# Two attentions around a routed expert layer on one core: start-up work as table steps, and keys and values of two more batches computed in the gaps between stages

## The chip, the cores and the metric

The kernel runs on one core of one Trainium2 chip. A core has five engines with instruction streams of their own: PE (matrix multiply; loading its weights is shown apart, as PEld), DVE (vector work along rows, which reads PE's results), ACT (functions, copies and scalings), POOL (a slower general engine, which also issues the indirect gathers and scatters), and SP (which issues transfers and computes nothing). Data sits in on-chip memory by partitions (up to 128 rows); PE writes its results to a small separate memory, PSUM, from which ACT or DVE copies them. Engines wait for each other through semaphores, and each engine runs its own instructions strictly in the order in which they were written into its stream.

The metric is device time in microseconds (us) of the whole program. Every time below is in microseconds from the start of the span, unless it says otherwise.

## The reference

There are 8 batches (B) of 112 rows (S) and 256 columns (D). Each batch has a context of 375 rows (SK). Four blocks follow each other, each added to x:

```
x = x + attention0(layernorm(x), ctx)        # 16 heads of 16, biases, softmax over 375 keys
x = x + experts(layernorm(x))                # router by distance in a ball, 2 of 8 experts per row
x = x + attention1(layernorm(x), ctx, mask)  # 16 heads, mask over 112 x 375, own weights
x = x + ffn(layernorm(x))                    # ternary weights, 1024 wide, convolution over 3 rows, silu

c_proj   = project_to_ball(centroids)
dot      = x_hyper @ c_proj.T
diff_sq  = max(x_norm_sq + c_norm_sq - 2 dot, 0)
arg      = 1 + 2 diff_sq / ((1 - x_norm_sq) (1 - c_norm_sq) + EPS)
top_v, top_i = top_k(-arccosh(arg), 2);   weights = softmax(top_v)
```

Two points matter for the change. The keys and values of both attentions are products of the same context with weights of each layer: `k1 = ctx @ Wk1`, `v1 = ctx @ Wv1` do not depend on x. They can be computed at any time once the context and the weights are on the chip. And the projected centroids and their norms depend on inputs alone.

## The kernel before

**Stages.** The kernel has four stages, one after the other, all in one instruction stream per engine. (1) Loads, and the attention of layer 0 with the router, for eight batches. (2) The experts: the routed rows lie sorted by expert in device memory (`tok`), and 19 tiles of 128 rows go through the two products of their expert (function `run`); the results go back to device memory (`ysc`). (3) The attention of layer 1; per batch it first gathers the two expert results of each row (`Gg0`, `Gg1`, L655) and adds them to x (`Dc0`, `Dc1`, L662). (4) The last feed-forward block.

**Steps and tables.** `attention(layer, ...)` (L622) defines the work of one batch as small named steps. The first letter of a name is the engine: P, D, A, G (POOL), S (SP). For one batch the order of data is: row statistics `Dbn`, `Dba`, `Grt`; normalisation `Dn` (L285); transposes `Ptn` (L703); queries `Ptq` (L716); keys `Pk0`, `Pk1` (L743, four matmuls each) with their copies `Aka0`, `Aka1`; values `Pv0` to `Pv2` (L763, four each in the trace) with copies `Ava0` to `Ava2` into the values' buffer; scores `Ps0` to `Ps3` (L789); the row maximum of the scores, `Dm00` to `Dm31` (L799 in layer 0, and L805 with the mask added in layer 1); then the scores once more in transposed form `Pp0` to `Pp2` (L842, L849), in layer 1 with the mask added by DVE (`Da00` to `Da21`, L860); the exponentials `Ae..` on ACT (L872); the weighted sums `Pw0`, `Pw1` (L887); and the output projection `Pto` to `Pout` (L936) with the addition to x, `Dx` (L940). Layer 0 goes on with the router's steps (`Drn`, `Ptg`, ..., `Dind`, `Prank`, `Drow`, `Gsc0`, `Gsc1`).

The order in which the engines get these steps is written out by hand in the table `ORDER`, one list per layer. An entry is a name, a time, and the first and last batch. Times are in units of one batch: a step with time t of batch b stands at b + t. The steps are sorted by that and issued:

```
plan = sorted((b + t, i, b, n) for i, (n, t, b0, b1) in enumerate(ORDER[layer]) for b in range(b0, b1 + 1))
with tc.manual_schedule(engines={ET.PE, ET.DVE, ET.Activation, ET.Pool}):
    for _, _, b, n in plan:
        do[n](b)
```

Inside it, PE, DVE, ACT and POOL take their instructions in just this order. SP is not in the list: its transfers are placed by the scheduler. So a step that waits for its data holds everything that the table puts behind it on its engine.

**Keys and values ahead.** `key_value(mark, batch, lay)` (L737) makes the steps of one batch's keys and values. With the mark `X0` and `X1` (`AHEAD = 2`) it makes those of layer 1 for batches 0 and 1; the table of layer 0 issues them near its end, with its last batch (7). Layer 1 computes the others, batches 2 to 7, in its own table (`Pk0 ... 2, 7`). The pool of keys and the list of values' buffers `vbuf` have three entries each; the buffers of values are filled with ones once, on POOL (L230), because each head's sum of weights comes out of such a column. The two small PSUM banks that hold keys, values, queries and transposes are handed out in turn by `misc`.

**Start.** Before the table of layer 0 the kernel issues, in program order, the loads (x and context of each batch by turns on SP, weights on ACT's queue), constants on POOL and DVE, the fills of the values' buffers, and the projection of the centroids (L303 to L316: one square, two matmuls, an inverse root, some ten small DVE steps). The mask's load is behind all of them on SP; DVE scales it by 1/16 (L997), a constant that the scheduler puts between the table's steps.

**Other work in the tables.** `Dtb0`, `Dta0`, `Ptc0`, `Dtc0`, `Dtd0`, `Dte0`, `Dtf0` (and the same with 1) make the ternary weights of the last block from loaded weights; the buffers of these raw weights are needed by two of the expert weights' loads, so those loads wait for `Dtf0` and `Dtf1`. `Sld` and `Slo` load layer 1's attention weights. `Glt0` to `Glt7` in layer 1's table build the convolution's diagonal matrices on POOL (L1111).

**The passage to the experts.** After the table of layer 0 come the last weights of the router and `rt.further()` (L526), which counts how many rows each expert has (L529) and picks the experts of the last tiles on DVE; with these, SP fetches the first tiles of rows (`tn`, L1033), which PE transposes (L1039).

## Time and profile before

| | us |
|---|---|
| median of three runs | 617.55 (617.51 to 618.69) |
| the profiled execution, its own time | 619.23 |
| span of the profiled execution | 617.5 |
| PE busy | 552.3 (89%) |
| DVE busy | 352.3 (57%) |
| ACT busy | 260.0 (42%) |
| POOL busy | 96.1 (16%) |

| stage, from its borders in the trace | from | to |
|---|---|---|
| loads, constants, first scores | 0 | about 30 |
| layer 0's attention and router in full swing | 30 | 190 |
| end of the router, count, first fetch (215.50) | 190 | 218 |
| experts | 218 | 362 |
| first gather (365.22), start of layer 1's attention | 362 | 410 |
| layer 1's attention | 410 | 538 |
| last block | 538 | 617.5 |

How to read it: the profile shows one execution. A line of the stage view gives, for a stretch of time, its length, and how long PE, PEld, DVE, ACT and POOL were busy in it (in brackets the number of instructions), then the mean granted clock of PE as a share of full speed, the busy share of the transfer engines and what they moved in GB/s. A line of the waits names an engine and its instruction, what it waited for, and the total, number and longest of these waits. A line of the timeline gives start, length, engine, line, operation, result and operands, and in square brackets how long the engine was idle before it and what it waited for. In the 40 slices each digit is a busy share in tenths of a slice of 15.4 us.

### The profile page before, as it was taken

What the parts mean: (1) busy time and instruction counts of PE and PEld (TensorE: products, weight loads), DVE (VectorE), ACT (ScalarE), POOL (GpSimd) and SP (SyncE); (2) the same over time, 40 slices, a digit from 0 to 9 for tenths busy, and PEclk for the clock granted to TensorE, in tenths of its full rate; (3) what the DMA queues carried; (4) which work ended last, traced back from release to release, by engine and by line L of the source; (5) the groups of instructions that cost most, each with busy time, mean ns of one, the idle gap of its engine ahead of it and who ended that gap; (6) DMA issues with size and microseconds to landing.
All of it is one profiled execution on the core that took longest, in us unless ns stands there. A gap on an engine that the chain in (4) does not pass through costs nothing. (4 is left out here: it accounts for less than half of the span.)

```text
span 617.5 us, 13564 instructions
## 1 busy us (share of the span) xinstructions
PE 552.3 (89%) x5402; PEld 418.5 (68%) x5402; DVE 352.3 (57%) x1093; ACT 260.0 (42%) x560; POOL 96.1 (16%) x185
## 2 busy tenths in 40 slices
PE   2799999999997689999999947799999999799983
PEld 1456666766685489998999934366666666588872
DVE  4464666787867601111111126889999989836653
ACT  1245565456462143333343311165454554554430
POOL 5000101223335300000000025323101201200000
PEclk9999999999999879999999985599999999989996
DMA  9999800021301039988889711000000000000000
GB/s 280 375 362 341 324 1 1 10 85 51 103 17 48 30 116 335 332 301 305 338 333 335 310 41 39 15 17 15 4 16 3 1 3 2 1 2 16 15 16 15
DMA packets 35916, 76.49 MB, mean 124 GB/s; under 512 B 3100, under 2 KB 29708, under 8 KB 30988
## 3 DMA queue, kind: packets, MB, share of 16 engines
q1 hardware_dynamic: 32940, 70.73, 32.2%
q0 software_dynamic: 1536, 3.67, 1.9%
q10 hardware_dynamic: 1376, 1.21, 0.7%
q8 instruction: 43, 0.70, 0.5%
q14 instruction: 21, 0.17, 0.1%
HBM read 55.68 MB, written 19.92 MB: 122 GB/s over the span
## 5 line engine op out<-in xcount | busy, mean ns | idle before, releaser
L1056 ACT ACTIVATE hT<-t_h,we 128x128 f32<-128x128 f32 x152 | 55.6, 368 | 82.0 <-PE t_h L1052 77.0
L1052 PEld LDWEIGHTS t_h<-tnT,we 128*128 128x128 f32 x608 | 80.1, 196 | 6.0 <-issue 0.6
L1052 PE MATMUL t_h<-tnT,we 128*128 128x128 f32 x608 | 83.5, 282 | 0.3 <-DMA we<-in_WA_dram 0.2
L799 DVE TENSOR_REDUCE topf<-pair 112x2 f32<-112x750 f32 x64 | 58.0, 930 | 36.1 <-PE pair L789 36.1
L789 PE MATMUL pair<-k,q 32*112 32x375 f32 x512 | 70.5, 551 | 5.5 <-DVE topf L799 3.2
L1063 PE MATMUL t_y<-we,hT 128*128 128x256 f32 x304 | 75.2, 380 | 0.0
L805 DVE CUSTOM_DVE_ANT_0 sm<-pair,mask 112x375 f32<-112x375 f32 x128 | 63.0, 540 | 7.9 <-PE pair L789 7.4
L842 PE MATMUL pair<-q,k 32*125 32x224 f32 x768 | 57.4, 376 | 1.1 <-DVE pT L860 0.8
L1063 PEld LDWEIGHTS t_y<-we,hT 128*128 128x128 f32 x304 | 53.3, 191 | 4.9
L860 DVE TENSOR_TENSOR pT<-pair,mask 125x896 f32<-125x896 f32 x48 | 50.6, 1085 | 7.1 <-PE pair L849 6.9
L763 PE MATMUL bank<-wv,ctx 128*125 128x256 f32 x192 | 51.8, 401 | 0.5 <-ACT k L756 0.3
L743 PE MATMUL bank<-ctx,wk 128*128 128x375 f32 x128 | 51.3, 526 | 0.0
L872 ACT ACTIVATE pT<-pair 125x896 f32<-125x896 f32 x48 | 42.5, 920 | 15.3 <-PE pair L849 15.1
L1041 DVE COPY tnT<-t_tn 128x256 f32<-128x256 f32 x19 | 8.1, 424 | 70.7 <-PE t_tn L1039 63.6
L682 POOL TENSOR_SCALAR rs<-mv 112x1 f32<-112x1 f32 x32 | 7.6, 237 | 251.4 <-DVE mv L676 204.6
L763 PEld LDWEIGHTS bank<-wv,ctx 128*125 128x125 f32 x192 | 33.3, 188 | 19.6 <-issue 6.7
L872 ACT ACTIVATE pT<-pT 125x896 f32<-125x896 f32 x48 | 45.6, 954 | 1.5 <-DVE pT L860 1.4
L887 PE MATMUL bank<-pT,v 125*32 125x112 f32 x1536 | 43.4, 261 | 0.0
L1065 DVE TENSOR_TENSOR y<-t_y,we 128x256 f32<-128x256 f32 x19 | 8.1, 425 | 60.1 <-PE t_y L1063 60.1
L1218 PE MATMUL t_c<-hpad,taps 128*128 128x224 f32 x192 | 40.5, 360 | 1.9 <-DVE hpad L1209 1.9
L842 PEld LDWEIGHTS pair<-q,k 32*125 32x125 f32 x768 | 31.4, 182 | 15.0 <-issue 4.4
L655 POOL DMA_INDIRECT yg<-ysc,at x16 | 16.7, 1045 | 156.6 <-SPq L1095 153.3
(206 smaller groups left out, 813.8 us busy)
## 6 DMA issues: line engine op xcount, KB each, us to landing
we<-in_WB_dram SPq DMA_DIRECT2D x19, 1152.0 KB, 7.2
we<-in_WA_dram SPq DMA_DIRECT2D x19, 1028.0 KB, 5.3
tok<-zero SPq DMA_DIRECT2D x8, 896.0 KB, 9.8
ysc<-zero SPq DMA_DIRECT2D x8, 896.0 KB, 10.6
ctx<-in_ctxT_dram SPq DMA_DIRECT2D x8, 375.0 KB, 5.8
tn<-tok SPq DMA_DIRECT2D x19, 128.0 KB, 5.9
ysc<-y SPq DMA_DIRECT2D x19, 128.0 KB, 3.0
we<-in_w1T_dram SPq DMA_DIRECT2D x1, 1024.0 KB, 7.6
```

What stands on the lines that cost most here:

```text
L743: nc.tensor.matmul(t, wts[lay]["k"][:, c, o * 128 : (o + 1) * 128], ctx_t[batch(b)][:, c, :], start=(c == 0), stop=(c == 1),)
L763: nc.tensor.matmul(t, ctx_t[batch(b)][:, c, i * KC : (i + 1) * KC], wts[lay]["v"][:, c, :], start=(c == 0), stop=(c == 1),)
L789: nc.tensor.matmul(ts[j // 2][:S, j % 2, :SK], q[r, c, i, :], k[r, c, :], start=True, stop=True)
L799: nc.vector.tensor_reduce(top[:, g, 2 * m : 2 * m + 2], t[:S, :, :SK], AX.X, ALU.max, negate=True)
L805: nc.vector.tensor_tensor_reduce(out=sm, in0=t[:S, n, :SK], in1=mask_t, scale=-1.0, scalar=3.0e38, op0=ALU.add, op1=ALU.min, accum_out=top ...
L842: nc.tensor.matmul(ts[j // 2][:KC, j % 2, n * 2 * S : (n + 1) * 2 * S], k[r, c, i * KC : (i + 1) * KC], q[r, c].rearrange("p i s -> p (i s)"),
L860: nc.vector.tensor_tensor(pT, st[b][f"p{s}"][m][:KC, :, : 4 * S], mask2[:, lo : lo + 4 * S].unsqueeze(1).to_broadcast([KC, 2, 4 * S]), ALU ...
L872: nc.scalar.activation(pT, src, AF.Exp)
L887: nc.tensor.matmul(po[32 * j : 32 * j + 32, g, :], v[:, i, h, :], st[b][f"T{s}{r // 2}"][:, r % 2, lo : lo + S], start=(i == 0), stop=(i = ...
L1052: nc.tensor.matmul(ph[:, i, :], w1[:, c, f * 128 : (f + 1) * 128], nt[:, c, :], start=(c == 0), stop=(c == 1),)
L1056: nc.scalar.activation(hT[:, f, :], ph[:, i, :], AF.Gelu, bias=b1[:, f : f + 1])
L1063: nc.tensor.matmul(py, hT[:, f, :], w2[:, f, :], start=(f == 0), stop=(f == NF - 1))
```

## The change

It has five parts.

1. **Four buffers.** `NKV = 4` keys and values are kept in place of three.
2. **Two more batches ahead.** `AHEAD = 3`: layer 1's keys and values of batch 2 (steps `PX2..` and `AX2..`) are issued on PE and ACT after `rt.further()`, in a manual schedule of their own, at the end of stage 1. Those of batch 3 (`PY..`, `AY..`) become the first steps of layer 1's table. The steps `Pk0` to `Ava2` of that table run over batches 4 to 7.
3. **Centroids as steps.** Their projection is taken apart into `Dce0`, `Pce`, `Dce1`, `Dce2`, `Dce3` of layer 0's table; their PSUM tile comes out of `misc`.
4. **Fills as steps.** The fill of each values' buffer is a step `Gms` (four of them, all before the first `Grt` on POOL).
5. **Both tables written anew.** All times in `ORDER` differ. Statistics of batches 0 to 5 stand ahead of the first normalisation; `Dbn2`, `Dba2`, `Grt2` come right after `Dx` in layer 0; the ternary steps `Dtf1` and `Dtf0` go from 7.76 and 6.67 to 9.52 and 9.93; in layer 1, gathers, normalisation and queries stand further ahead of the scores. A tile of statistics has a tag per batch.

The diff, the tables cut to rows that the text speaks of:

```diff
+NKV = 4
...
 ORDER = [
     [
-        ("Dbn", -0.7765, 0, 7), ("Dba", -0.7547, 0, 7), ("Grt", -0.6335, 0, 7), ("Dn", -0.5744, 0, 7),
-        ("Ptn", -0.4938, 0, 7), ("AnT", -0.4537, 0, 7), ("Dtb1", -0.0374, 4, 4), ("Pk0", 0.0988, 0, 7),
-        ("Aka0", 0.1715, 0, 7), ("Ptq", 0.1943, 0, 7), ("Pk1", 0.2299, 0, 7), ("Aq0", 0.2348, 0, 7),
...
-        ("Ae20", 2.6258, 0, 7), ("Ae21", 2.6435, 0, 7), ("Pw0", 2.6710, 0, 7), ("Au0", 2.7427, 0, 7),
-        ("Dtf1", 2.7640, 5, 5), ("Gxb", 2.8424, 0, 7), ("Pw1", 2.9085, 0, 7), ("Au1", 3.0470, 0, 7),
...
-        ("AoT", 3.4147, 0, 7), ("Dte0", 3.5660, 3, 3), ("Pout", 3.6431, 0, 7), ("Dtf0", 3.6728, 3, 3),
-        ("Dx", 3.7361, 0, 7), ("Dbn2", 3.7658, 0, 7), ("Dba2", 3.8311, 0, 7), ("Grt2", 3.9219, 0, 7),
-        ("PX0k0", 4.0016, 7, 7), ("Drn", 4.0321, 0, 7), ("AX0ka0", 4.1799, 7, 7), ("Ptrn", 4.2797, 0, 7),
...
-        ("Dwt3", 8.1115, 0, 6), ("PX1v0", 8.3020, 7, 7), ("Dwt4", 8.9238, 0, 6), ("PX0v1", 9.1727, 7, 7),
-        ("AX1va0", 9.9255, 7, 7), ("PX1v1", 9.9306, 7, 7), ("AX0va1", 10.9247, 7, 7), ("PX1v2", 12.5746, 7, 7),
-        ("AX1va2", 13.3041, 7, 7), ("AX1va1", 13.3187, 7, 7),
+        ("Gms", -13.7779, 0, 3), ("Dbn", -6.4648, 0, 7), ("Dba", -4.7943, 0, 7), ("Dce0", -1.7910, 0, 0),
+        ("Pce", -1.7313, 0, 0), ("Grt", -1.4128, 0, 7), ("Dn", -1.0660, 0, 7), ("Dce1", -0.9077, 0, 0),
+        ("Dce2", -0.8237, 0, 0), ("Ptn", -0.5250, 0, 7), ("AnT", -0.4788, 0, 7), ("Dbv", -0.3448, 0, 0),
+        ("Pk0", 0.0228, 0, 7), ("Aka0", 0.1009, 0, 7), ("Ptq", 0.1418, 0, 7), ("Aq0", 0.1524, 0, 7),
+        ("Aq1", 0.1538, 0, 7), ("Dtb1", 0.1883, 4, 4), ("Pk1", 0.2718, 0, 7), ("Aka1", 0.3455, 0, 7),
...
+        ("Dce3", 3.5143, 0, 0), ("Pout", 3.6425, 0, 7), ("Dta0", 3.8385, 2, 2), ("Dtd0", 3.8469, 3, 3),
+        ("Dx", 3.8562, 0, 7), ("Dbn2", 3.8849, 0, 7), ("Dba2", 3.9033, 0, 7), ("Sld", 3.9228, 7, 7),
...
+        ("Dte0", 4.4070, 3, 3), ("Ptxh", 4.5004, 0, 7), ("Dtf1", 4.5188, 5, 5), ("PX0k1", 4.6075, 7, 7),
...
+        ("AX0va2", 6.7018, 7, 7), ("Gsc0", 6.7050, 0, 7), ("Gzp", 6.7086, 0, 6), ("Dtf0", 6.9259, 3, 3),
...
+        ("AX1ka1", 11.1606, 7, 7), ("PX1v0", 12.6658, 7, 7), ("AX0va1", 15.1426, 7, 7), ("AX1va0", 16.2566, 7, 7),
+        ("PX1v1", 18.7421, 7, 7), ("PX1v2", 21.1829, 7, 7), ("AX1va1", 21.4854, 7, 7), ("AX1va2", 21.5325, 7, 7),
     ],
     [
-        ("Glt2", -1.5527, 2, 2), ("Glt4", -0.8856, 3, 3), ("Gg0", -0.8478, 0, 7), ("Gg1", -0.0270, 0, 7),
-        ("Dc0", 0.1031, 0, 7), ("Dc1", 0.6929, 0, 7), ("Dbn", 0.8581, 0, 7), ("Dba", 0.9380, 0, 7),
-        ("Grt", 1.0255, 0, 7), ("Dn", 1.1608, 0, 7), ("Ptn", 1.4147, 0, 7), ("AnT", 1.4394, 0, 7),
-        ("Ptq", 1.4946, 0, 7), ("Glt1", 1.5354, 1, 1), ("Aq0", 1.6034, 0, 7), ("Aq1", 1.6114, 0, 7),
-        ("Pk0", 1.6690, 2, 7), ("Aka0", 1.8455, 2, 7), ("Pk1", 1.8699, 2, 7), ("Pv0", 1.9181, 2, 7),
-        ("Aka1", 1.9194, 2, 7), ("Ava0", 1.9673, 2, 7), ("Pv2", 2.0318, 2, 7), ("Ava2", 2.0662, 2, 7),
...
-        ("AoT", 5.3602, 0, 7), ("Glt6", 5.4852, 4, 4), ("Pout", 5.5954, 0, 7), ("Dx", 5.7841, 0, 7),
-        ("Dbn2", 6.3743, 0, 7), ("Dba2", 6.6812, 0, 7), ("Grt2", 18.6197, 0, 7),
+        ("PYk0", -7.5045, 0, 0), ("AYka0", -6.5223, 0, 0), ("PYv0", -4.1792, 0, 0), ("PYk1", -3.5149, 0, 0),
+        ("AYka1", -3.0547, 0, 0), ("Gg0", -2.9094, 0, 7), ("AYva0", -2.8470, 0, 0), ("Glt4", -2.6415, 3, 3),
+        ("Gg1", -2.2704, 0, 7), ("Dc0", -2.1626, 0, 7), ("Dc1", -2.0232, 0, 7), ("Dbn", -1.6276, 0, 7),
+        ("Dba", -1.4959, 0, 7), ("PYv2", -1.3473, 0, 0), ("PYv1", -1.1210, 0, 0), ("Glt2", -1.1172, 2, 2),
+        ("Pk0", -0.8862, 4, 7), ("Grt", -0.8791, 0, 7), ("Dn", -0.8401, 0, 7), ("AYva2", -0.8185, 0, 0),
+        ("Aka0", -0.7755, 4, 7), ("AYva1", -0.7108, 0, 0), ("Ptn", -0.5306, 0, 7), ("AnT", -0.4737, 0, 7),
+        ("Ptq", -0.0442, 0, 7), ("Aq0", 0.0956, 0, 7), ("Aq1", 0.1186, 0, 7), ("Pk1", 0.1410, 4, 7),
+        ("Pv0", 0.2416, 4, 7), ("Aka1", 0.2572, 4, 7), ("Ava0", 0.2849, 4, 7), ("Pv1", 0.3637, 4, 7),
...
+        ("Dbn2", 3.8996, 0, 7), ("Glt5", 4.0090, 3, 3), ("Glt0", 4.2437, 1, 1), ("Dba2", 4.3336, 0, 7),
+        ("Grt2", 4.5365, 0, 7),
     ],
 ]
...
-    kp = ctx.enter_context(tc.tile_pool(name="keys", bufs=3))
+    kp = ctx.enter_context(tc.tile_pool(name="keys", bufs=NKV))
...
-    vbuf = [kp.tile([KC, NKC, H, 2 * A], F32, tag="v", name="v") for _ in range(3)]
-    for v in vbuf:
-        nc.gpsimd.memset(v, 1.0)
+    vbuf = [kp.tile([KC, NKC, H, 2 * A], F32, tag="v", name="v") for _ in range(NKV)]
...
-    with tc.tile_pool(name="ps_c", bufs=1, space=PSUM) as ps_c, tc.tile_pool(name="cent", bufs=1) as ep:
+
+    def centroids(ap, misc):
+
+        c_ = {}
         cent = col("cent", 0, 2 * E).rearrange("p (c e) -> p c e", c=2)
-        csq = ep.tile([128, 2, E], F32, tag="csq", name="csq")
-        nc.vector.tensor_mul(csq, cent, cent)
-        t = ps_c.tile([128, E], F32, tag="t", name="t_c")
-        for c in range(2):
-            nc.tensor.matmul(t, ones, csq[:, c, :], start=(c == 0), stop=(c == 1))
-        nc.vector.tensor_copy(cn, t)
-        cs, cc = ep.tile([128, E], F32, tag="cs", name="cs"), ep.tile([128, E], F32, tag="cc", name="cc")
-        nc.vector.tensor_scalar_max(cc, cn, 1e-14)
-        rsqrt(cc, cs, E, "ball")
-        nc.vector.tensor_scalar(cs, cs, 0.95, 1.0, ALU.mult, ALU.min)
-        nc.vector.tensor_mul(cproj, cent, cs.unsqueeze(1).to_broadcast([128, 2, E]))
-        nc.vector.tensor_mul(cn, cn, cs)
-        nc.vector.tensor_mul(cn, cn, cs)
-        nc.vector.tensor_scalar_min(cn, cn, 0.99)
-        nc.vector.tensor_scalar(cn1, cn, -1.0, 1.0, ALU.mult, ALU.add)
+        V = nc.vector
+
+        def square(b):
+            c_["sq"] = csq = ap.tile([128, 2, E], F32, tag="csq", name="csq")
+            V.tensor_mul(csq, cent, cent)
+
+        def norms(b):
+            c_["t"] = t = misc("t_c")[:, :E]
+            for c in range(2):
+                nc.tensor.matmul(t, ones, c_["sq"][:, c, :], start=(c == 0), stop=(c == 1))
+
+        def get(b):
+            V.tensor_copy(cn, c_.pop("t"))
+            c_["c"], c_["s"] = [ap.tile([128, E], F32, tag=n, name=n) for n in ("cc", "cs")]
+            V.tensor_scalar_max(c_["c"], cn, 1e-14)
+
+        def root(b):
+            rsqrt(c_["c"], c_["s"], E, "ball")
+
+        def into(b):
+            cs = c_["s"]
+            V.tensor_scalar(cs, cs, 0.95, 1.0, ALU.mult, ALU.min)
+            V.tensor_mul(cproj, cent, cs.unsqueeze(1).to_broadcast([128, 2, E]))
+            V.tensor_mul(cn, cn, cs)
+            V.tensor_mul(cn, cn, cs)
+            V.tensor_scalar_min(cn, cn, 0.99)
+            V.tensor_scalar(cn1, cn, -1.0, 1.0, ALU.mult, ALU.add)
+
+        return {"Dce0": square, "Pce": norms, "Dce1": get, "Dce2": root, "Dce3": into}
...
-    AHEAD = 2
+    AHEAD = 3
...
-                    st[b]["bn"] = t = sp.tile([S, 6], F32, tag=f"bnst{i}", name="bnst")
+                    st[b]["bn"] = t = sp.tile([S, 6], F32, tag=f"bnst{b}", name="bnst")
...
-                            d["v"] = vbuf[made[0] % 3]
+                            d["v"] = vbuf[made[0] % NKV]
...
                 for n in range(AHEAD):
                     key_value(f"X{n}", lambda b, n=n: n, 1)
+            else:
+                key_value("Y", lambda b: AHEAD, 1)
...
                 do.update(ternary(misc))
+                do.update(centroids(ap, misc))
+                do["Gms"] = lambda b: nc.gpsimd.memset(vbuf[b], 1.0)
...
                 res = rt.further()
+
+                n = AHEAD - 1
+                with tc.manual_schedule(engines={ET.PE, ET.Activation}):
+                    for i in range(2):
+                        do[f"PX{n}k{i}"](B - 1)
+                        do[f"AX{n}ka{i}"](B - 1)
+                    for i in range(NKC):
+                        do[f"PX{n}v{i}"](B - 1)
+                        do[f"AX{n}va{i}"](B - 1)
```

## The prediction

> **What bounds the kernel now.** I read the page's 40 slices first, then busy time cut at the stage borders, then the waits of DVE and PE inside the stages that the change touches, and single pieces of the timeline last. The slices:
>
> ```profile
> PE   2799999999997689999999947799999999799983
> DVE  4464666787867601111111126889999989836653
> PEclk9999999999999879999999985599999999989996
> ```
>
> PE is full almost everywhere. The holes lie at the start, about slice 14 (between the first attention and the experts), at slice 24 (between the experts and the second attention) and late. In two places the granted clock (PEclk) falls. The stages:
>
> ```profile
> core 0: us, PE busy (x) PEld busy (x) DVE busy (x) ACT busy (x) POOL busy (x), PEclk, DMA share, GB/s
> 30.00:190.00 160.00, 157.72 (x2036) 109.19 (x2035) 111.44 (x359) 87.85 (x183) 33.85 (x54) 0.99 0.37 128
> 190.00:218.00 28.00, 17.90 (x82) 12.77 (x82) 18.28 (x126) 5.72 (x17) 11.12 (x14) 0.86 0.16 52
> 218.00:362.00 144.00, 143.45 (x950) 132.30 (x948) 15.96 (x38) 56.84 (x153) 0.00 (x0) 0.98 0.78 289
> 362.00:410.00 48.00, 31.65 (x183) 17.24 (x183) 31.92 (x95) 9.14 (x17) 18.25 (x25) 0.68 0.09 27
> 410.00:510.00 100.00, 100.00 (x1303) 65.46 (x1302) 93.41 (x282) 51.70 (x98) 15.57 (x24) 1.00 0.03 9
> ```
>
> Layer 0 and the experts are PE's alone. From 410 on PE and DVE are both near full, so taking work from PE alone gains only down to DVE's own time. Between 362 and 410 PE is slow, not full. The waits of PE up to 218, and then of DVE and PE from 364 to 540:
>
> ```profile
> PE t_tn L1039 <- DMA tn<-tok: 6.7, 1, 6.7
> ...
> DVE sm L805 <- PE pair L789: 7.4, 10, 2.7
> DVE pT L860 <- PE pair L849: 6.9, 10, 1.2
> ...
> PE bank L703 <- DVE n L285: 13.5, 2, 11.1
> ```
>
> The profiled execution took 619.23, its span 617.5, so 1.73 lies around the span; the median of the runs is 617.55, 1.68 below the profiled one. I sum against the span, add 1.73, and take 1.68 off.
>
> **Part 1, the start.** The new table puts the row statistics of batches 0 to 5 ahead of the first normalisation n(0) on DVE. x5 is issued on SP at 9.84 and lands about 5.1 later (rows of its neighbours), so n(0) starts at about 15.4 where it started at 12.12: +3.3. The centroids' first steps, now DVE and PE steps of the table, stand behind the same waits. What covers the 3.3 is the mask:
>
> ```profile
> 21.21 0.94 DVE L799 TENSOR_REDUCE topf<-pair 112x2 f32<-112x750 f32 x1 [6.53 <-PE pair L789]
> ...
> 25.53 0.35 DVE L997 TENSOR_SCALAR mask<-mask 112x375 f32<-112x375 f32 x1 [3.38 <-DMA mask<-in_mask_dram]
> ```
>
> DVE has its first score maximum done at 22.15 and then waits 3.38 for a load that the change leaves where it was. A first maximum done at 25.45 still ends before 25.53; my walk, with the centroid steps gone from ahead of it, gives 24.2. After that DVE has less to do, since the statistics are done. I take −0.8, between −2 and +1.5; without the cover it is +3.3. The four fills of the values' buffers (1.34 each on POOL) go behind the identity and the constants; POOL is 8.87 busy of 30, and the nearest reader is a copy at about 17: 0.
>
> **Part 2, the middle of layer 0.** Same instructions on PE, 157.72 of 160 busy: 0, from −1 to +4 if the new order stalls it. The ternary weights' last steps (1.22 to 1.27 each on DVE) come later, and two expert loads behind them on SP move from 134 and 156 to some 170 to 190. Behind them on SP stand only the later weights and the first fetches of tokens (215.50). Each takes 5.3 to 7.2 to land and is read at 228 at the earliest: 0, with 30 to spare.
>
> **Part 3, from layer 0 to the experts.** Batch 2's keys and values of layer 1 (two key steps, L743 x4 at 1.26 to 1.46; three value steps, L763 x4 at 1.06: about 6) now stand on PE and ACT behind the router's last count. The chain that sets the end runs from the last rank over the count (210.57), DVE's chosen list (215.2) and SP's fetch (215.50) to the transposes of 217.66; it waits for none of the new work. One value step that held the count moves behind it: −0.4. PE, which idled 6.70 here, now works through 6.1 to 6.5 of it, and the transposes wait at most 0.5 for the last copy out of PSUM. The gain is the clock:
>
> ```profile
> 217.00:224.00 7.00, 6.29 (x29) 5.74 (x30) 0.85 (x2) 2.53 (x5) 0.00 (x0) 0.52 0.28 79
> ```
>
> The first 5.9 of the experts ran at half clock; kept warm they take half, −3.0, less part of the wait of 0.5: −2.6, between −3 and −0.5 (late fetches of tn could hold it).
>
> **Part 4, the experts.** The same instructions, 143.45 of 144 on PE: 0.
>
> **Part 5, into layer 1.** Batch 3's five steps fill PE from 362.3 to about 369.5. The first gather still waits for the last write of the experts (365.22), and the first normalisation for the gather, so the first scores stand where they did (first masked maximum at 378.12): 0 by itself. If PE's new steps ran late they would hold the first transposes, behind which the first scores are queued; they end 3 ahead of them. That idle time of about 3.0 (before: some 10) matters for the clock. In this trace it fell 5.75 after PE's work ended in this same place (367.45), but 2.8 after it at 213.76, so by the nearest row it falls again, and the sum goes by half clock. [...]
>
> **Part 6, the ramp.** In before, batch 2's transposes wait 2.42 for n(2) at 389.6 to 392 with the scores of batch 1 queued behind them; then batch 2's queries (2.01 at half clock) and first key step (2.39) stand ahead of the next scores, while DVE waits 2.69 and 1.12 until
>
> ```profile
> 403.06 1.09 DVE L860 TENSOR_TENSOR pT<-pair,mask 125x896 f32<-125x896 f32 x1 [1.12 <-PE pair L849]
> ```
>
> In the new table neither stands there. Walking it at half clock with DVE's rows (0.47 a masked maximum) I reach this instruction at about 396.7, −6.4; the queries and n(2) come back later at about 1.4: −5.0.
>
> **Part 7, the steady part.** A batch costs DVE about 17.5 (16 maxima at 0.47, 6 mask additions at 1.04, some 3.7 of small ones). PE needs 13.4 without keys and values and 13.4 + 5.7 = 19.1 with them; the ends of successive batches lie 18.0 to 18.9 apart. Two of the six batches with their keys and values in the loop lose them, so DVE's 17.5 sets their slots: −1.0 each, −2.0. Against it: PE is then about 77% busy there, and the clock dipped in before when PE waited (387.8); I put +1.5. Parts 6 and 7 give −5.5. The bounds: 0 if DVE's waits only change their place; and about −10, since DVE is busy for 150.0 of the 176 from 362 to 538 (31.92 + 93.41 + 24.7) and needs some 16 of the other 26 for the gather before its first maximum and for the drain after its last. The middle is right by another row too: DVE's waits for PE there are 7.4 + 6.9 = 14.3, of which those behind keys and values that stay in the loop (batches 4 to 7) remain.
>
> **Part 8, the last stage.** Its order is the same: 0.
>
> Sum: −0.8 − 0.4 − 2.6 − 5.5 = −9.3; span 608.2, profiled 609.9, median about 608.3.
>
> **Rivals.** (a) *PE falls to half clock in the slots without keys and values: slower.* Until batch 4's first key step comes in (about 397 to 425) PE has 13.4 of work in 17.5. The rows speak both ways: the clock fell after a stretch about 65% busy (384.4 to 387.8) and stayed up through one of about 78% (401 to 404.5). If it falls, a slot costs PE 26.8 against 18.5, and 1.6 slots make +13: 608.3 + 13 ≈ 621. It decides as soon as PE's waits reach about a third of some stretch of 3 to 4. [...] 0.25.
> (b) *The clock stays up into layer 1*, by the 5.75 of part 5 against its 2.8. Of the 6.1 that DVE waits for scores from 372 to 410, about half goes: 605.3. 0.10.
> (c) *Layer 1 does not shorten:* a wait for n(1) or the gathers takes the place of the queries, DVE being 93% busy anyway. 608.3 + 5.5 = 613.8. 0.14.
> (d) *The start's cover fails* (a later x5, or the mask addition not last): 3.3 more, 611.6. 0.07.
> (e) *Gains and stalls cancel* within 0.2% (1.2, about what a measurement of this kernel can tell from no change). 0.04.
>
> **How the numbers follow.** The forecast has 0.40, on its own 605 to 611.5. Faster is the forecast with (b), (c) and (d), 0.71; same 0.04; slower 0.25. The range goes from 603.5, where (b) lies with 1.8 to spare, to 621, the middle of (a); outside are half of (a), 0.12, and some 0.05 below.
>
> **What would show it.** n(0) at about 15.4 and the mask still at 25.5; PE busy from 211 to 217 and a clock near 1.0 from 217 to 224; the experts' end about 4 earlier; the first mask addition some 6 less after the first maximum than the 24.9 of before; ends of batches 17.5 apart where no key step lies between. It is wrong if the clock reads 0.5 to 0.7 between first scores and batch 4's keys, if PE shows new waits in layer 0, or if the fetch of the tokens comes later than the chosen list.

## The result, and the profile after

The changed kernel takes 613.62 us (median of 20 executions, 610.3 to 621.03) against 618.83 for the kernel before (20 executions, 617.51 to 622.7). The ratio is 0.9912, 95% interval 0.9894 to 0.993: faster by 0.9%. Ratios and their intervals leave out executions more than 1.5% above the fastest of their kernel, the medians are over all. The forecast was 608.3 against a median of 617.55, that is 1.5%; the measured median lies above the 605 to 611.5 that the forecast gave itself. The spread matters for reading the traces: seven of the 20 executions of the changed kernel lie above 615, with a mean granted clock of 0.937 to 0.947, and the others below it, with 0.953 to 0.962. The profiled one took 612.15, its span is 610.4 (before 619.23 and 617.5).

The slices of the changed kernel:

```profile
PE   0899999999997889999999987989999999899983
DVE  2564655787878611111111107889999998846653
PEclk9999999999999999999999996579999999899996
```

Counted from 0, the two dips of the clock before the experts (slices 13 and 14) are gone, the hole at slices 23 to 25 is mostly filled, but the clock is still low from 24 to 26. The stages (the same cuts as before, and the experts' first 7 us):

```profile
core 0: us, PE busy (x) PEld busy (x) DVE busy (x) ACT busy (x) POOL busy (x), PEclk, DMA share, GB/s
30.00:190.00 160.00, 156.91 (x2042) 107.61 (x2040) 112.06 (x362) 87.48 (x180) 33.05 (x49) 1.00 0.38 128
190.00:218.00 28.00, 22.75 (x110) 16.12 (x110) 17.89 (x123) 7.95 (x21) 11.04 (x14) 1.00 0.18 57
218.00:362.00 144.00, 141.46 (x939) 128.97 (x939) 15.28 (x36) 56.32 (x153) 0.00 (x0) 1.00 0.80 288
362.00:410.00 48.00, 41.06 (x255) 23.02 (x253) 35.32 (x119) 12.90 (x23) 22.13 (x29) 0.65 0.12 35
410.00:510.00 100.00, 98.27 (x1326) 64.18 (x1322) 93.17 (x272) 50.33 (x90) 11.36 (x23) 1.00 0.02 4
217.00:224.00 7.00, 6.66 (x55) 6.16 (x55) 0.42 (x1) 5.28 (x13) 0.00 (x0) 1.00 0.27 78
```

From 217 to 224 the clock is 1.00 where it was 0.52. From 362 to 410 PE does more (41.06 in place of 31.65) at a clock that is no better: 0.65 against 0.68. The waits of PE and DVE that answer to those shown of before (PE up to 220, DVE and PE from 360 to 540):

```profile
PE t_tn L1074 <- DMA tn<-tok: 1.4, 2, 1.1
...
DVE sm L829 <- PE pair L813: 8.2, 12, 1.3
DVE pT L884 <- PE pair L873: 5.3, 7, 2.6
...
PE bank L725 <- issue: 3.4, 1, 3.4
```

PE's 6.7 before the experts is 1.4, its 11.1 before layer 1 is 3.4. DVE's waits for PE in layer 1 hardly changed in sum: 13.5 against 14.3. The pieces of DVE's timeline that mark the start and layer 1's ramp:

```profile
23.02 0.94 DVE L823 TENSOR_REDUCE topf<-pair 112x2 f32<-112x750 f32 x1 [4.00 <-PE pair L813]
25.96 0.35 DVE L1032 TENSOR_SCALAR mask<-mask 112x375 f32<-112x375 f32 x1 [2.01 <-DMA mask<-in_mask_dram]
376.49 0.55 DVE L829 CUSTOM_DVE_ANT_0 sm<-pair,mask 112x375 f32<-112x375 f32 x1 [0.53 <-PE pair L813]
395.00 1.09 DVE L884 TENSOR_TENSOR pT<-pair,mask 125x896 f32<-125x896 f32 x1 [0.86 <-PE pair L873]
```

Cut at events instead of at fixed times, the difference of the two spans adds up:

| stretch, by its events | before | changed | difference |
|---|---|---|---|
| start to the mask's scaling | 25.53 | 25.96 | +0.43 |
| to the last `Dx` of layer 0 | 164.89 | 163.70 | −1.19 |
| to the first transposes of the experts | 27.24 | 26.08 | −1.16 |
| to the experts' last y | 144.09 | 144.55 | +0.46 |
| to layer 1's first masked maximum | 16.37 | 16.20 | −0.17 |
| to its first mask addition | 24.94 | 18.51 | −6.43 |
| to its last `Dx` | 134.38 | 136.66 | +2.28 |
| to the end | 80.06 | 78.74 | −1.32 |
| span | 617.5 | 610.4 | −7.1 |

Below, "layer 1" is the time from the first masked maximum to its last `Dx` (159.32 before, 155.17 changed), and the ramp is its part up to the first mask addition. These are single executions, and the two differ by more than the medians do (7.1 against 5.2), since the profiled one of before lies 0.4 above its median and that of the changed kernel 1.5 below its own. The first line follows the arrival of loads (25.5 to 27.9 over all profiles of this study), so the experiments are compared by stretches, and medians against runs of the kernel before on the same chip. The second line varies too. Ten traces have the same steps up to there, the changed kernel's and those of the nine experiments that keep its table of layer 0. From the mask to the `Dx` of batch 6 all ten take 155.5 to 155.8 (before 156.92), but to the last `Dx` four take 163.6 to 163.7, the changed kernel's among them, and six take 165.6 to 166.0; in these six the clock fell to 0.5 between 186 and 189.

### The profile page after: what moved, and what is told of

Same layout as the page of the kernel before. It is cut to its first block, busy times and chain, and to the rows that moved or that the text cites. A ratio compares the mean times of both kernels' runs of the same rounds, so it can differ in the third digit from the quotient of the medians.

```text
span 610.4 us, 13549 instructions
## 1 busy us (share of the span) xinstructions
PE 555.3 (91%) x5402; PEld 416.9 (68%) x5402; DVE 347.9 (57%) x1093; ACT 261.7 (43%) x560; POOL 98.3 (16%) x186
## 5 line engine op out<-in xcount | busy, mean ns | idle before, releaser
L1087 PEld LDWEIGHTS t_h<-tnT,we 128*128 128x128 f32 x608 | 77.6, 191 | 8.3 <-ACT hT L1091 1.8
L1087 PE MATMUL t_h<-tnT,we 128*128 128x128 f32 x608 | 81.9, 279 | 1.4 <-DMA we<-in_WA_dram 0.8
L813 PE MATMUL pair<-k,q 32*112 32x375 f32 x512 | 75.5, 570 | 4.1 <-DVE pT L884 1.9
L829 DVE CUSTOM_DVE_ANT_0 sm<-pair,mask 112x375 f32<-112x375 f32 x128 | 64.5, 561 | 8.3 <-PE pair L813 8.2
L866 PE MATMUL pair<-q,k 32*125 32x224 f32 x768 | 60.6, 381 | 1.8 <-DVE pT L884 0.8
L785 PE MATMUL bank<-wv,ctx 128*125 128x256 f32 x192 | 49.8, 390 | 1.9 <-ACT k L778 0.8
L765 PE MATMUL bank<-ctx,wk 128*128 128x375 f32 x128 | 48.4, 506 | 1.7 <-DVEq L1130 1.1
L911 PEld LDWEIGHTS bank<-pT,v 125*32 125x32 f32 x1536 | 36.8, 111 | 11.8 <-issue 3.6
L813 PEld LDWEIGHTS pair<-k,q 32*112 32x112 f32 x512 | 25.3, 186 | 28.7 <-issue 8.3
L866 PEld LDWEIGHTS pair<-q,k 32*125 32x125 f32 x768 | 32.9, 185 | 16.6 <-issue 5.0
## 6 DMA issues: line engine op xcount, KB each, us to landing
ysc<-zero SPq DMA_DIRECT2D x8, 896.0 KB, 11.1
```

What stands on the lines that cost most here:

```text
L765: nc.tensor.matmul(t, wts[lay]["k"][:, c, o * 128 : (o + 1) * 128], ctx_t[batch(b)][:, c, :], start=(c == 0), stop=(c == 1),)
L785: nc.tensor.matmul(t, ctx_t[batch(b)][:, c, i * KC : (i + 1) * KC], wts[lay]["v"][:, c, :], start=(c == 0), stop=(c == 1),)
L813: nc.tensor.matmul(ts[j // 2][:S, j % 2, :SK], q[r, c, i, :], k[r, c, :], start=True, stop=True)
L829: nc.vector.tensor_tensor_reduce(out=sm, in0=t[:S, n, :SK], in1=mask_t, scale=-1.0, scalar=3.0e38, op0=ALU.add, op1=ALU.min, accum_out=top ...
L866: nc.tensor.matmul(ts[j // 2][:KC, j % 2, n * 2 * S : (n + 1) * 2 * S], k[r, c, i * KC : (i + 1) * KC], q[r, c].rearrange("p i s -> p (i s)"),
L911: nc.tensor.matmul(po[32 * j : 32 * j + 32, g, :], v[:, i, h, :], st[b][f"T{s}{r // 2}"][:, r % 2, lo : lo + S], start=(i == 0), stop=(i = ...
```

## The experiments

**Parts one by one.** In the first, the old table of layer 0 is put into the changed kernel:

```diff
-        ("Gms", -13.7779, 0, 3), ("Dbn", -6.4648, 0, 7), ...
+        ("Gms", -13.7779, 0, 3), ("Dce0", -5.0, 0, 0), ("Pce", -4.99, 0, 0), ("Dce1", -4.98, 0, 0),
+        ("Dce2", -4.97, 0, 0), ("Dce3", -4.96, 0, 0),
+        ("Dbn", -0.7765, 0, 7), ...            # the list of before
```

> The changed kernel with the old table of layer 0 (centroids and fills stand ahead of it, as before); keys and values stay moved and layer 1 keeps its new table. Theory (each gain sits in its own stage): the 0.8 by which batch 7 of layer 0 ends earlier and some 1.2 more up to the fetch of tokens are lost, the clock at the experts' start and the shorter ramp of layer 1 stay: span +2, about 612.4, fetch of tokens at about 215.5. Rival (the early part of the gain comes from the moved keys and values alone, the new layer-0 table brings nothing): fetch at about 213.5, span unchanged at 610.4.

Measured: 616.77 against 620.82 (ratio 0.994, 0.9914 to 0.9966). From the mask to the end of layer 0 it takes 166.24, with first transposes at 220.04. The end is no fair mark, since kernels with the new table reach 166.0 there as well. To the `Dx` of batch 6 it takes 158.34, against 155.5 to 155.8 in all ten traces with the new table, so layer 0's new table is worth something, more than expected. But the price is not clean: the scheduler put the mask's scaling (27.39) ahead of the first maximum (27.66), which no table had asked for, and in the medians the two kernels' intervals overlap. And layer 1, whose table and steps are the changed kernel's, took 157.92 in place of 155.17, with the clock at 0.5 from 375 up to 415 (in the changed kernel from 369.8 to 397.1 and from 403.95 to 410.8). So one and the same table differs by 2.7 beside another course of the clock.

Then the moved keys and values alone, in the old tables:

```diff
+NKV = 4
-    AHEAD = 2
+    AHEAD = 3                                   # and the PX2 steps after rt.further()
+        ("PYk0", -7.5045, 0, 0), ..., ("AYva1", -1.7108, 0, 0),
-        ("Pk0", 1.6690, 2, 7), ...
+        ("Pk0", 1.6690, 4, 7), ...
```

> The kernel before with the keys and values of batches 2 and 3 moved into the two gaps (four buffers), both tables otherwise as before. Theory: the experts start at full clock (third transposed tile about 1.6 earlier against the fetch), part of that is lost again in the experts' stage; in layer 1 the first key step of batch 2 (2.39) no longer stands ahead of the first mask addition, but n(2) and the queries of batch 2 still do: first maximum to first mask addition about 22 instead of 24.9; span about 614 to 615. Rival (moved keys and values alone carry the change): span about 611, first mask addition 18.5 after the first maximum.

Measured: 624.88 against 620.82, ratio 1.0038 (1.0006 to 1.0069): slower. Both theories missed it. About 4 of its profiled execution comes from stage 1, where the mask again went ahead of the first maximum (26.89 before 27.16; end of layer 0 at 194.83 in place of 190.42). Most of the rest is layer 1: 163.00 in place of 159.32, although two batches' keys were gone. Between 414 and 444 the clock falls twice; before, it read 1.00 over the same 30:

```profile
414.00:420.00 6.00, 5.62 (x62) 3.27 (x62) 4.09 (x15) 1.64 (x3) 1.28 (x2) 0.50 0.15 41
...
432.00:438.00 6.00, 4.17 (x45) 2.23 (x45) 5.93 (x14) 1.20 (x2) 3.86 (x4) 0.71 0.14 40
438.00:444.00 6.00, 6.00 (x58) 3.55 (x47) 3.26 (x15) 2.75 (x6) 0.00 (x0) 0.72 0.00 0
```

That the moved keys are the reason is argued here; the fillers below test it.

The reverse, both new tables with the keys back in the loop:

```diff
-    AHEAD = 3
+    AHEAD = 2                                   # no PX2, no PY steps
-        ("Pk0", -0.8862, 4, 7), ...
+        ("Pk0", -0.8862, 2, 7), ...
```

> The changed kernel with both new tables, but keys and values of batches 2 and 3 back in layer 1's loop. Theory: the experts start at half clock again (loses 1.6), the ramp of layer 1 has two more batches of keys and values on PE at half clock (each 5.7 at full, 11 at half clock), so that the first mask addition comes 24 or more after the first maximum: span about 615 to 618. Rival (the new tables carry the change): span about 611 to 612.

Measured: 619.57 against 620.82, ratio 0.9986 (0.9959 to 1.0012): no difference that can be told. The span of 615.0 is the theory's, but not for its reason: the ramp is 19.07, not 24. So in these traces it is the new order that brings most of the −6.43; but layer 1 is 158.41 all the same. The comparison is not at one clock: over the first 40 of layer 1 the clock is 0.82 with the keys in the loop and, as shown below, 0.66 without. Neither half alone makes the kernel faster.

**What ate the lead in the experts.** Their first y comes 13.23 after the first transposes, not 14.85: the warm clock is worth 1.62. At the last y nothing of it is left. Slow weights were the first suspicion:

```diff
+            m = n if w is WA else n // 2
+            nc.sync.dma_start(out=t[:, :m], in_=w[e, :, :m] ...)
```

> The changed kernel with half of the second weights of each expert loaded (the other half of the product uses the same half again, the added bias is another row of the weights, so the experts' result is not the reference's; the number of instructions is the same). It takes 576 KB of some 2.2 MB from each of 19 tiles. Theory (the lead of the experts' warm start is lost since their weights come at the pace of the transfers): from the first transposes to the last y 141 to 142.5 in place of 144.55, no wait for weights on PE. Rival (PE alone paces the experts): 144 to 145.

Measured: 615.74 against 619.0 (ratio 0.9947, 0.9917 to 0.9978); the stretch took 145.43 with no wait for weights left on PE, longer than both theories had it. In the changed kernel PE waits for weights twice, before once:

```profile
PE t_h L1087 <- DMA we<-in_WA_dram: 0.8, 2, 0.5
```

```profile
PE t_h L1052 <- DMA we<-in_WA_dram: 0.2, 1, 0.2
```

So these waits explain 0.6 of the lost lead. Whether slow weights cost more than that, the run with half loads can't tell cleanly, as its order of instructions in this stage is a third one. The distances between the y of the last tiles are: 6.14, 6.35, 5.24 before (17.73), 6.13, 4.56, 7.91 in the changed kernel (18.60). All ten other kernels with moved keys and full loads have 18.60 to 18.81; the one with the new tables and the keys in the loop has 17.73. In the instruction order the experts' transposes, hidden products and outputs are interleaved otherwise: their order is the scheduler's, not a table's, and it changed though no line of them did. That is 0.87. The rest lies in single tiles that take 0.2 to 1.2 more than their neighbours; the two waits for weights of 0.3 and 0.5 stand at some of them. Their share isn't settled, and the stretch varies: in the eleven traces with the changed order and full loads it takes 143.05 to 145.52. Nor is the warm start safe: in the three traces that have moved keys and the old table of layer 0, the clock fell for 3.4 between 221 and 227, and the first y came 14.1 to 14.3 after the first transposes.

**The clock of layer 1.** In the changed kernel PE's work before layer 1 ends at 367.8, its next begins at 371.2, and the clock falls in between:

```profile
367.00:369.80 2.80, 0.78 (x4) 0.35 (x2) 1.85 (x5) 0.70 (x2) 2.16 (x4) 1.00 0.33 99
369.80:371.20 1.40, 0.00 (x0) 0.02 (x1) 0.90 (x3) 0.00 (x0) 1.13 (x3) 0.51 0.31 82
```

This stretch was filled with idle work first:

```diff
+WARM = 4
+    for _ in range(WARM):                       # a step after PYv1
+        nc.tensor.matmul(pairs[0][:, 0, :SK], wts[1]["k"][:, 0, 0:128], ctx_t[0][:, 0, :], start=True, stop=True)
```

> The changed kernel with four idle matmuls (about 2.9, results never read) behind batch 3's last value step on PE, in the 3.43 in which PE idles before the first transposes of layer 1. Theory (the half clock of the ramp is caused by this idle stretch, and the ramp is PE's alone at half clock, 18.5 busy of 18.5): clock near 1.0 from 368 to 394, first maximum about 1.5 earlier, first mask addition about 16.5 after it instead of 18.5, span 3 to 4 less, about 607. Rival 1 (DVE sets layer 1 whatever the clock): clock near 1.0 but span 609.5 to 610.4. Rival 2 (the clock falls for another reason): clock still 0.5 from 370, span unchanged.

Measured: 614.77 against 620.82, ratio 0.9912 (0.9879 to 0.9945), as the changed kernel's; the 3 to 4 less did not come. The clock stays up until 376.3, the first maximum comes 15.46 after the last y (16.20 in the changed kernel), and then, with PE 9.81 busy of the next 10.2, the clock reads 0.5. The fall comes 13.3 after the last y. In the nine traces that have batch 3's keys in front of the idle stretch and leave it empty, it comes 9.5 to 12.1 after it. That fits the idle stretch as the reason of the first fall, without proving it, and something else keeps the clock down. Two pairs test what. Fillers of equal number, place and columns, with 128 or with 32 rows of the array (in these two kernels, and in the one with the old tables further down, they write beside live sums in the two small banks, and the values are not the reference's):

```diff
+    for j in range(2):                          # 18 steps between 0.45 and 3.0 of layer 1's table
+        nc.tensor.matmul(banks[j % 2][:, 384:512], wts[1]["k"][0:128, 0, 0:128], ctx_t[0][0:128, 0, 0:128], ...)
                                                 # second kernel: [0:32, ...] in both operands
```

> The changed kernel with 18 fillers (two idle matmuls of 128 rows by 128 columns each, about 0.6 at full clock, never read) spread over PE's part of layer 1's table from the first scores to batch 4's first key step. They do the reverse of what moving keys and values did: they give PE full-array work in the slots that lost it. Theory (with the keys gone, PE's activity in these slots is too low and the clock falls there, in some executions for longer): clock nearer 1.0 from about 395 to 417, layer 1 shorter by 1 to 4 than the 155.2 of the changed kernel, and the spread of the executions narrower (610 to 621 before). Rival (the half clock does not cost anything because DVE is the bound): layer 1 longer by 0 to 3, since 10 of PE work are added.

> As the filler run before it, with the same number and length of idle matmuls, but with 32 rows of the array in place of 128. If the clock follows how long PE is busy, it does what the filler of 128 rows does. If it follows how much of the array works, the clock stays at 0.5 to 0.8 up to 417 and layer 1 is longer than in the changed kernel, by some 2 to 5.

And the same question with twelve larger matmuls that go where the next scores overwrite them:

```diff
                     st[b][f"s{g}"] = ts = [pair("sc"), pair("sc")]
+                    if layer == 1 and b <= 2:
+                        nc.tensor.matmul(ts[0][:, 0, :SK], wts[1]["k"][:, 0, 0:128], ctx_t[0][:, 0, :], ...)
                                                 # control: [0:32, ...] in both operands
```

> The changed kernel with one idle matmul of 128 rows by 375 columns (about 0.73 at full clock) before each score step of batches 0 to 2 in layer 1, 12 in all, into the place that the scores then overwrite, so that nothing else is touched. Theory (the clock follows how much of the array works, and scores use 32 rows): clock 1.0 from about 381 to 417, first maximum to first mask addition about 16.7 in place of 18.5, first batch's end about 1.9 nearer to the first maximum; layer 1 shorter than 155.2 by up to 1.9 where no dip falls into its drain, and fewer executions above 615. Rival (the half clock is hidden behind DVE): layer 1 155 to 156, median as the changed kernel's.

> As the run with twelve idle matmuls before the scores of batches 0 to 2, with the same number, columns and places, but 32 rows of the array in place of 128. Theory (the clock follows how much of the array works): clock 0.5 to 0.8 from 372 to 417, first maximum to first mask addition 20 or more in place of 15.7, layer 1 158 to 164, slower than the changed kernel. Rival (any work on PE keeps the clock up, or the order that the twelve force is what helps): clock 1.0 from 381, layer 1 151 to 153.

Each of the next lines is the 40 us from the first masked maximum on, in the view of stages. The kernel before, then the new tables with the keys in the loop:

```profile
378.12:418.12 40.00, 35.48 (x261) 19.93 (x262) 33.19 (x109) 13.14 (x24) 9.77 (x14) 0.75 0.06 18
```

```profile
377.44:417.44 40.00, 39.06 (x342) 23.40 (x342) 34.03 (x119) 13.63 (x25) 11.34 (x16) 0.82 0.08 24
```

The changed kernel:

```profile
376.49:416.49 40.00, 38.30 (x338) 22.28 (x338) 34.54 (x121) 12.23 (x21) 11.91 (x16) 0.66 0.08 24
```

The 18 fillers of 128 rows, then of 32 rows:

```profile
377.30:417.30 40.00, 39.72 (x418) 26.68 (x420) 36.59 (x123) 12.66 (x22) 11.69 (x16) 0.98 0.09 24
```

```profile
377.53:417.53 40.00, 39.28 (x250) 28.06 (x253) 29.21 (x104) 9.68 (x15) 10.52 (x16) 0.54 0.07 20
```

The twelve of 128 rows, then of 32 rows:

```profile
379.88:419.88 40.00, 38.25 (x400) 21.68 (x400) 39.60 (x133) 15.71 (x26) 11.84 (x16) 1.00 0.08 24
```

```profile
380.32:420.32 40.00, 39.96 (x216) 24.05 (x220) 28.96 (x102) 9.81 (x15) 10.93 (x16) 0.50 0.07 20
```

PE is "busy" for 38 to 40 of 40 in the last five. The clock (third figure from the right) is 0.98 and 1.00 with 128 rows, 0.54 and 0.50 with 32, and PE got 400 matmuls done against 216. Before it was 0.75, so it was low in this stretch already; without the keys it is 0.66. DVE, next to it, is busy 39.60 or 28.96 in the last two: with the clock at 1.00 it is the bound here, with 0.50 PE is (39.96).

| kernel | first maximum to mask addition | layer 1 | median, ratio to before |
|---|---|---|---|
| changed | 18.51 | 155.17 | 613.62, 0.9912 |
| 18 fillers, 128 rows | 16.71 | 154.99 | 615.95, 0.9936 (0.9903 to 0.9969) |
| 18 fillers, 32 rows | 23.42 | 166.25 | 624.64, 1.0091 (1.0062 to 1.012) |
| 12 before scores, 128 rows | 15.66 | 151.11 | 611.68, 0.9865 (0.9821 to 0.9909) |
| 12 before scores, 32 rows | 22.66 | 163.95 | 621.95, 0.9994 (0.996 to 1.0028) |

The profile of the last row (624.3) is one of that kernel's longer executions, which reach from 614.7 to 633.2. The pairs don't hang on it: of either pair every execution with 128 rows is faster than every one with 32 (609.6 to 618.8 against 622.9 to 627.2; 606.1 to 613.6 against 614.7 to 633.2; the second pair ran on two chips, where the kernel before has medians of 618.8 and 618.9). Adding about 9 of work to PE (an estimate: in the trace of the twelve of 128 rows from the start of one to that of its scores is 0.72 to 0.83 at a clock of 1.00) made layer 1 shorter by 4 with 128 rows, and longer by 9 in the profiled execution with 32. The 18 fillers did less than expected: the clock rose to 0.98, but layer 1 stayed at 154.99, and the executions spread from 609.6 to 618.8 still.

What the pairs show is that the height of the idle matmuls decides here: 0.98 against 0.54, and 1.00 against 0.50. That the scores keep the clock down because each uses 32 rows is a reading beyond that. In the changed kernel's 40 us, 80 score matmuls of 0.808 each, 64.6 in sum, take 19.9 together, so by these records about three run at once (an estimate), each in 32 rows of its own by the code:

```profile
L813 PE MATMUL pair<-k,q 32*112 32x375 f32 x80 | 19.9, 808 | 1.0 <-DVE pT L884 1.0
```

How many rows work at a time, and what about them the clock follows, stays open.

In the old tables the filler did not rescue the moved keys:

> The kernel with keys and values moved and the old tables (which ran slower than the kernel before, layer 1 163.0 against 159.3, with the clock at 0.5 to 0.9 in parts from 414 to 444), with 21 of the same 128-row fillers in layer 1 from the first scores to batch 4's keys. Theory (it is slower because the clock falls in the slots that lost their keys): clock 1.0 from 410 on, layer 1 back to 155 to 159. Rival (the old order stalls without its keys): layer 1 stays at 163 or grows.

Measured: 622.35 against 619.0, ratio 1.0053 (1.003 to 1.0075); layer 1 161.90. The clock was more often up (0.88 over the first 62 us in place of 0.72; 0.5 was left up to 388, from 398 to 405 and from 435 to 439), yet DVE waited for scores as long as without it. First the kernel with moved keys, then with fillers, in the waits of DVE over 62 us from the first maximum:

```profile
DVE sm L811 <- PE pair L795: 10.9, 7, 2.5
```

```profile
DVE sm L819 <- PE pair L803: 11.1, 8, 3.2
```

So the rival holds at least in part: the old order stalls without its keys, with the clock at 0.72 as at 0.88, and the clock is not the whole of that kernel's loss. How much is one and how much the other stays open, as the fillers are work too.

**Useful work as filler, and both fillers together.** Batch 3's five steps moved from the stretch before layer 1 to between the first scores:

```diff
-        ("PYk0", -7.5045, 0, 0), ..., ("PYv1", -1.1210, 0, 0),
+        ("PYk0", 0.6000, 0, 0), ("PYk1", 0.9500, 0, 0), ("PYv0", 1.3000, 0, 0), ("PYv1", 1.5500, 0, 0), ("PYv2", 1.8000, 0, 0),
```

> The changed kernel with the five steps of batch 3's keys and values taken out of the stretch before layer 1 and spread between the scores of batches 0 and 1 (useful work of 128 rows in place of idle matmuls). Theory (full-array work in the ramp keeps the clock up): clock up to 1.0 by about 385, first mask addition 17.5 to 19 after the first maximum although 5.7 of work more stands in the ramp, layer 1 about 155, span equal to the changed kernel's within 1. Rival (only the amount of PE work in the ramp counts): first mask addition 24 after the first maximum as in the kernel before, layer 1 159 to 161.

Measured: 614.98 against 618.81, ratio 0.995 (0.9913 to 0.9987); clock 1.00 from 384 to 402, first mask addition 18.31, layer 1 155.02. PE had 5.7 more to do in the ramp than in the changed kernel and layer 1 lost nothing by it. The whole kernel is no faster than the changed one by its ratio. Then the four idle matmuls and the twelve in one kernel:

> Both idle pieces together, the four matmuls in the stretch before layer 1's first transposes and the twelve before the scores of batches 0 to 2. Theory: the clock stays at 1.0 through the ramp, the first maximum comes 0.7 nearer to the first gathered rows (15.5 after the last y in place of 16.2) and the first mask addition 16 to 16.5 after it; span about 2 under the changed kernel's in the same state of the start, median about 0.991 times 0.997 of before. Rival (DVE is the bound): as the run with the twelve alone.

Measured: 609.53 against 618.81, ratio 0.9832 (0.9795 to 0.9869), the lowest median of the study. Its interval lies below the changed kernel's and overlaps that of the twelve alone (0.9821 to 0.9909), so what the four add is seen in the traces only. Its clock in the slices never leaves the top from the experts' start to the last slice:

```profile
PEclk9999999999996899999999999999999999999997
```

First maximum 15.60 after the last y, mask addition 15.64 after it, layer 1 149.43, 5.7 less than in the changed kernel; the last block takes 77.2 (78.74 in the changed kernel, with the clock at 0.5 from 530 to 537). The expected 16 to 16.5 and "2 under" were too cautious.

## Why the prediction was right or wrong

The direction held, and the mechanism up to layer 1's first mask addition; the size was 9.3 forecast and 7.1 in the profiled execution, 5.2 between medians. The median of 613.62 lies near the 613.8 of rival (c), but that is chance: layer 1 did shorten, by 4.15.

- **Part 1, right.** n(0) went to 14.82 (forecast 15.4), the end of the first maximum to 23.96 (24.2), and the mask still ended DVE's wait, 0.43 later by its own arrival. Layer 0's end moved by −0.76 (−0.8). That it fits so closely is partly luck: in six of the ten traces with the same steps the last batch ends 2 later after the mask, with the clock at 0.5.
- **Part 2, right** on PE (156.91 of 160) and on the two late loads, issued at 179 and 184; PE's waits for weights stand at 297 and 328.
- **Part 3, chain undersized, clock term wrong in the end.** Up to the first transposes −1.16 where −0.4 stood. The clock rose as forecast, 1.62 by the first y against 2.6, and nothing of it reached the last y. The step that failed is part 4's "the same instructions: 0": they were, but in another order, whose last three tiles took 0.87 longer.
- **Part 5, right.** The idle time came out at 3.43 (3.0), the clock fell, the first maximum came 0.17 nearer. Rival (b) didn't happen: the clock fell at 369.8, 2.0 after PE's work ended, sooner than after the 2.8 and the 5.75 that the forecast read in the trace of before. (The prediction read the two falls of before some 0.3 late; they stand at 367.1 and 213.5, that is 5.4 and 2.6 after PE's work.)
- **Part 6, right to the digit.** −6.43 against −6.4 at half clock. What comes back later was mis-sized: 2.28 from the first mask addition to the last `Dx`, where parts 6 and 7 together had 0.9.
- **Part 7, wrong.** The four distances from the first to the fifth batch's end took 74.30 (73.63 before), not 2 less. The step that failed is "two of the six batches with their keys and values in the loop lose them: −1.0 each". The steps moved away had run from 399.5 to 411 and from 417 to 428, all ahead of the first end (438.1), so between the ends there was nothing for them to free: with the new tables and the keys in the loop the four distances are 74.23, and 73.63 with moved keys and the old tables. The first batch ended earlier, but with the table's steps shifted DVE had more left behind it: from the fifth end to the last it was busy 25.64 in place of 22.36, and took 30.43 in place of 25.66. The right measure is the whole layer: 159.32 to 155.17, −4.15 where −5.5 stood. DVE's idle time in it went only from 16.41 to 15.47. Its busy time went from 142.91 to 139.70, mostly since one normalisation, n(2), took 2.41 before, beside POOL's fills (the other five, and all six now, 0.40), and one addition of an expert's result 1.18 in place of 0.48. So "DVE's waits only change their place", the lower bound, was nearly true.
- **Part 8, not nothing.** The last block took 1.32 less with its order unchanged. The clock was at 0.5 for 6.8 at its start before, and for 5.4 now; whether that is all of it isn't settled.
- **Rival (a) was at work inside the forecast.** The clock was low through the slots without keys (0.66 over 40 us, 0.75 before), as it said. What it got wrong is the cause, "waits of a third of some stretch": at 38.30 of 40 busy PE was hardly waiting. And it need not be a separate branch: some executions may pay more of it than others, which may be why seven of 20 lie above 615. No trace of one of them was taken, and the fall at the end of layer 0, beside which the last batch ends 2 later, may have its part. The two kernels with 128-row fillers before the scores have none above 613.7 in six each.

## What to carry to other kernels

When work is moved out of a loop to relieve PE, ask what else it did there. Here the keys and values were matmuls over 128 rows between scores of 32 rows each, 8.2 of PE's first 40 in layer 1 before and none after (the queries, 5.2 and 5.1, stayed). Without them the clock read 0.66 in place of 0.75, and with it held up the kernel gained 1.7% in place of 0.9%. Read the granted clock beside the busy share, stage by stage; where it is low at a full busy share, try a few idle matmuls over all 128 rows: here twelve of them, about 9 of work, made layer 1 shorter by 4. And a stage whose order a scheduler chooses has to be compared in its order, even if not a line of it was touched.

## What was not expected

That PE's busy time does not tell the clock, and that the height of a few idle matmuls does: the clock stayed at 0.50 for 40 us with PE busy for 39.96 of them, and at 1.00, with PE busy for 38.25, when the twelve idle ones among its matmuls were four times as tall. Between these scores "busy" is not enough. The steps are coarse, too: the stretches at half clock ahead of the program's end last 3.41, 3.42, 10.24, 17.06, 13.66 and 6.82 in the trace of before, 27.31, 6.83 and 6.83 in that of the changed kernel, each within 0.03 of a whole multiple of 3.41. And neither moving the keys nor the tables paid alone: moved keys 1.0038 (its profiled execution lost some 0.006 in stage 1, in the order that the scheduler gave its start), new tables 0.9986, both 0.9912.
